# Where five residual loads stand in ScalarE's queue: ahead of the left scan instead of behind its first steps, in layer 1 of a scan-convolution kernel

## The chip, the cores and the metric

One Trainium2 chip, one of its cores. The metric is the device time of one execution in microseconds (us). The kernel before takes 4293.07 us, the median of 3 runs (4291.05 to 4299.52). The core has five engines that run by themselves: TensorE (PE), VectorE (DVE), ScalarE (ACT), GpSimd (POOL) and SyncE (SP). SP and ACT also issue the DMAs here, each in its own order.

## The reference

The input is x, 32 images of 48 channels, 64 rows and 128 columns, float32. Two layers of the same form follow each other; each adds to x a chain of four scans over the group-normalised x.

```python
x = x + conv_ref(_gn(x), down_w, down_b, right_w, right_b, left_w, left_b)

def conv_ref(x, ...):
    # one step of a scan: nxt = inp + conv1d(carry, w, b), 5 taps, 48 -> 48 channels
    D = scan down the rows of x          # 63 steps, conv along the columns
    U = scan up the rows of D            # 63 steps, the same weights
    R = scan right over the columns of U # 127 steps, conv along the rows
    L = scan left over the columns of R  # 127 steps
    return L
```

A step needs the one before it, so the work is a chain of 2 x (2 x 63) steps per image by rows and 2 x 127 by columns and layer.

## The kernel before, in words

The 32 images are four groups of 8. The work is cut into twelve phases (`PHASES`): a phase by rows scans one group down and up (126 steps), a phase by columns scans a pair of groups right and left (254 steps). The order is written out by hand; layer 1 is phases 4 and 7 to 11. Phase 9 is `rows` of layer 1, group 3; phase 10 is `cols` of layer 1, pair 0; phase 11, the last, is `cols` of layer 1, pair 1. Here are 8 x 126 + 4 x 254 = 2024 steps in a row. A step is nine products on PE (`step`, L741) and three additions on DVE, each from PSUM with the bias and the new input, in place into the arena (L750).

The arena in SBUF has three slots and four further tiles (`stage`). A phase by columns works on quarters of 32 columns: a quarter is loaded (`load_unit`, from the DRAM tiles `upa`/`upb`, into which the phase by rows moved its up-going rows with `move_rows`) in six units, 20 DMAs in all. A unit is 128 partitions by 2048 elements, 1 MB, and takes 3 or 4 DMAs, as it is put together from the pieces of several column offsets. Quarters 0, 1 and 2 have a slot each; quarter 0 is spilled to DRAM (`spill_unit`) when it is done, quarter 3 takes its slot, and quarter 0 is brought back in the left scan.

In the left scan a quarter's result is final for this layer when the scan has passed it. Then, unit by unit, POOL adds the residual (`add_residual`, L673), POOL and ACT copy the sum in another order of elements into the tile that held the residual (`permute_unit`, L698), and the tile is stored to the output, or in phase 10 for three quarters to a DRAM tile `held` (`hold_result`, on ACT's queue), from which it goes to the output in phase 11 (`let_result`, on SP's). The residual of a unit is read by `load_residual` from the DRAM tiles `mid`, in layer 1 on ACT's queue, into a ring of tiles: the four stage tiles and one (`spare_tiles[0]`), in the last phase two, that lies in the tile `early`. There it lies on the weights of the phases by rows (`down1`), which are in use up to the end of phase 9; the second lies on the weights of the right scan.

What sets the order. Each piece of work is put on an agenda with a due step (`at(t, fn, ...)`); before each scan step all that is due is issued, in order of due step, by `in_order`, which ties the instructions of each engine into one fixed order. For phase 10 or 11, `t0` is the step at which it begins, `left = t0 + 127` the first step of its left scan. A tie by order is not a time: an instruction runs when its engine has come to it and its waits are over, so ACT, which is not busy in layer 1's right scans, can be far ahead of the steps. In `plan_cols` stands therefore, at `left + 10`, a copy of a single element by ACT (`nc.scalar.copy` to `junk`, shown in the profile under L240) that reads a column which the left scan writes in its seventh step; what is behind it on ACT has to wait for that. The first residual units are put on the agenda at `left + 16`, behind it.

Each DMA of SP and ACT counts up one of eight completion counters, in turn, as the scheduler that builds the program places them. A later DMA on the same counter is issued only when the one before it has landed.

Of the kernel before, what the change touches and what calls it, by code (L numbers as in the profile page):

```python
# [120 lines left out]
def kernel(  # L121
# [508 lines left out]
    def quarter(k, j):  # L630
        return slot[slots(k)[j % 3]].rearrange("p (o s n) -> p s o n", s=2, o=NG)
# [188 lines left out]
    def at(t, fn, *args):  # L820
        agenda.append((t, len(agenda), fn, args))
# [66 lines left out]
    def plan_cols(k, t0, prev):  # L888
        _, layer, pair = PHASES[k]
# [24 lines left out]
        left = t0 + W - 1  # L914
# [20 lines left out]
        for u, (t, j, i) in enumerate(direct):  # L935
            nat = tiles[u % n]
            o, half = UNITS[i]
            if u < n:
                at(left + 16, load_residual, k, j, i, nat)
            if layer == 0:  # L940
                if u >= n:
                    at(direct[u - n][0] + 3, load_residual, k, j, i, nat)
                at(t, add_residual, k, j, i, nat)
                at(t + 4, keep_result, k, j, i)
                unit = quarter(k, j)[:, half, o]
                if half == 0:
                    for b in range(GB):
                        at(t + 5 + b, stats[0].take, j, o, unit, b)
                else:
                    at(t + 1, stats[1].take, j, o, unit)  # L950
            else:

                at(t, add_residual, k, j, i, nat)
                at(t + 2.5, permute_unit, k, j, i, nat, (nc.gpsimd, nc.scalar, nc.scalar))
                if final or j not in HELD:
                    at(t + 4.5, store_result, k, j, i, nat)
                else:
                    at(t + 4.5, hold_result, j, i, nat)
                if final and j == 1:
                    at(t + 4.7, load_residual, k, 0, i, last_tiles(k)[i])  # L960

                if u >= 2 and u - 2 + n < len(direct):
                    at(t + 4.6, load_residual, k, *direct[u - 2 + n][1:], tiles[(u - 2) % n])
# [15 lines left out]
    def last_tiles(k):  # L979

        s = slot[slots(k)[2]].rearrange("p (i n) -> p i n", i=2 * NG)
        return [s[:, i] for i in range(2 * NG)]
# [13 lines left out]
    for k, (kind, layer, _) in enumerate(PHASES):  # L996
        (plan_rows if kind == "rows" else plan_cols)(k, starts[k], PHASES[k - 1][0])
# [211 lines left out]
```

## Time and profile before

| | |
|---|---|
| median of 3 runs | 4293.07 us (4291.05 to 4299.52) |
| the profiled execution, its own time | 4290.3 us |
| its span, first to last instruction | 4288.2 us |
| mean granted clock of PE | 0.981 |
| `arena<-mid` on ACT's queue, 384 KB | 76 DMAs, 9.3 us to landing |
| `early<-mid` on ACT's queue, 384 KB | 20 DMAs, 12.8 us to landing |
| `arena<-upb` on SP's queue, 384 KB | 96 DMAs, 12.3 us to landing |

Times are from the span's start. "Busy" is the time in which an engine has an instruction; a queue (SPq, ACTq) is the issuing side of an engine, and a line of it gives the start, the time up to the last issue, and the number of DMAs. Behind an arrow stands what ended a wait. In a table of stretches the last columns are the granted PE clock, the mean busy share of the 16 DMA engines (a little over 1 is possible) and what they moved in GB/s.

### The profile page before, as it was taken

Reading aid. Unit: us, or ns where it says so; the run is one execution under the profiler, and the core shown is the slowest. Engines: PE = TensorE matmul, PEld = TensorE weight load, DVE = VectorE, ACT = ScalarE, POOL = GpSimd, SP = SyncE. Lnnn points to the kernel's source line nnn. Section 1 sums busy time; section 2 is a strip of 40 time slices with the busy share of each in tenths; the row PEclk is TensorE's granted clock in tenths of the full one; section 3 lists DMA queues with packets and bytes.
Section 4 is the critical chain, followed back from the end, with each engine's and each line's share of the span. In section 5 each row is a group of like instructions: output and inputs, shape, how many; then the busy total and the mean of one; then the engine's idle time right before and its main releaser. Section 6 shows DMA issues by size and latency. Waiting matters only on the chain. (4 is left out here: it accounts for less than half of the span.)

```text
span 4288.2 us, 89979 instructions
## 1 busy us (share of the span) xinstructions
PE 4058.9 (95%) x36648; PEld 4029.3 (94%) x36648; DVE 2164.5 (50%) x6503; ACT 1340.1 (31%) x2662; POOL 886.2 (21%) x906
## 2 busy tenths in 40 slices
PE   3699998999999999998999999999999999999992
PEld 1699998999999999998999999999999999999992
DVE  6345444446664444444446654444444444444443
ACT  1584301435793564100006772613000002210122
POOL 4271001325323020010005310000000024510352
PEclk9899999999999999999999999999999999999996
DMA  9599799857998979679308979939289049999999
GB/s 213 113 216 162 105 167 168 245 127 213 230 198 156 163 140 160 103 127 206 85 1 242 222 154 149 148 50 161 43 140 200 1 78 247 247 243 156 180 202 182
DMA packets 2116733, 680.12 MB, mean 159 GB/s; under 512 B 2005440, under 2 KB 2056160, under 8 KB 2076384
## 3 DMA queue, kind: packets, MB, share of 16 engines
q1 hardware_dynamic: 2015904, 581.64, 70.2%
q10 hardware_dynamic: 97216, 86.44, 9.9%
q0 software_dynamic: 3200, 6.30, 0.5%
q8 instruction: 288, 4.72, 0.5%
q14 instruction: 125, 1.02, 0.1%
HBM read 397.38 MB, written 295.98 MB: 162 GB/s over the span
## 5 line engine op out<-in xcount | busy, mean ns | idle before, releaser
L614 ACT ACTIVATE arena<-arena,offset,scale 128x256 f32<-128x256 f32 (+2 forms) x816 | 575.6, 801 | 432.9 <-DMA arena<-mid 176.1
L673 POOL TENSOR_TENSOR arena<-arena 128x2048 f32<-128x2048 f32 x80 | 363.1, 4553 | 1386.0 <-PE step_10l L741 434.1
L569 POOL COPY arena<-arena 96x256 f32<-96x256 f32 x448 | 265.0, 650 | 553.8 <-DMA arena<-in_x 444.2
L512 ACT ACTIVATE early<-arena 128x256 f32<-128x256 f32 x192 | 129.4, 674 | 477.2 <-POOL arena L673 471.2
L741 PE MATMUL step_00r<-arena,early 128*128 128x128 f32 x2286 | 251.5, 274 | 14.1 <-DMA arena<-upa 14.1
L741 PEld LDWEIGHTS step_00r<-arena,early 128*128 128x128 f32 x2286 | 251.1, 185 | 14.5 <-issue 14.4
L741 PE MATMUL step_01r<-arena,early 128*128 128x128 f32 x2286 | 250.6, 273 | 14.4 <-DMA arena<-upa 14.4
L741 PEld LDWEIGHTS step_01r<-arena,early 128*128 128x128 f32 x2286 | 250.4, 185 | 14.6 <-issue 14.5
L741 PE MATMUL step_11r<-arena,early 128*128 128x128 f32 x2286 | 251.3, 273 | 8.2 <-DVE arena L750 8.2
L741 PEld LDWEIGHTS step_11r<-arena,early 128*128 128x128 f32 x2286 | 250.8, 185 | 8.7 <-DVE arena L750 8.6
L741 PE MATMUL step_00l<-arena,wleft 128*128 128x128 f32 x2286 | 249.1, 272 | 0.0
L741 PEld LDWEIGHTS step_00l<-arena,wleft 128*128 128x128 f32 x2286 | 248.6, 184 | 0.0
L741 PE MATMUL step_10l<-arena,wleft 128*128 128x128 f32 x2286 | 248.5, 272 | 0.0
L741 PE MATMUL step_11l<-arena,wleft 128*128 128x128 f32 x2286 | 248.5, 272 | 0.0
L741 PE MATMUL step_01l<-arena,wleft 128*128 128x128 f32 x2286 | 248.4, 272 | 0.0
L741 PE MATMUL step_10r<-arena,early 128*128 128x128 f32 x2286 | 248.4, 272 | 0.0
L741 PEld LDWEIGHTS step_10l<-arena,wleft 128*128 128x128 f32 x2286 | 248.4, 184 | 0.0
L741 PEld LDWEIGHTS step_11l<-arena,wleft 128*128 128x128 f32 x2286 | 248.4, 184 | 0.0
L741 PEld LDWEIGHTS step_01l<-arena,wleft 128*128 128x128 f32 x2286 | 248.4, 184 | 0.0
L741 PEld LDWEIGHTS step_10r<-arena,early 128*128 128x128 f32 x2286 | 248.4, 184 | 0.0
L698 ACT COPY arena<-arena 128x256 f32<-128x256 f32 x172 | 99.7, 656 | 411.5 <-POOL arena L673 162.2
L240 ACT COPY early<-arena 128x1 f32<-128x1 f32 x2 | 0.4, 191 | 657.9 <-DVE arena L750 657.9
(189 smaller groups left out, 7171.3 us busy)
## 6 DMA issues: line engine op xcount, KB each, us to landing
arena<-in_x SPq DMA_DIRECT2D x24, 1536.0 KB, 11.6
xin<-arena SPq DMA_DIRECT2D x96, 384.0 KB, 4.7
arena<-xin SPq DMA_DIRECT2D x96, 384.0 KB, 8.5
mid<-arena SPq DMA_DIRECT2D x96, 384.0 KB, 7.8
arena<-mid SPq DMA_DIRECT2D x192, 192.0 KB, 4.2
upb<-arena SPq DMA_DIRECT2D x192, 192.0 KB, 3.9
arena<-upb SPq DMA_DIRECT2D x96, 384.0 KB, 12.3
arena<-xin SPq DMA_DIRECT2D x186, 192.0 KB, 4.3
```

The lines of the kernel that those rows point to most:

```text
L240: fn(*args)
L512: nc.scalar.activation(junk[:, 0:n], view[:, b], AF.Identity, accum_out=self.sum[:, i, j : j + 1])
L569: copy(dst[:, r, q], src[:, r0 + r, q])
L614: nc.scalar.activation(args[0], args[0], AF.Identity, bias=args[2], scale=args[1])
L673: eng.tensor_tensor(unit, unit, nat, ALU.add)
L698: copy(by_w(perm)[:, a], src[:, a])
L741: nc.tensor.matmul(part(whole(ps[o])[0:m], -s), weights[:, i, at : at + m], part(src(i), s), start=seen[o] == 1, stop=seen[o] == left[o],)
```

## The change

In layer 1 the first five residual units of each left scan get another due step: unit u of 0 to 4 is due at `left - 44 + 4 * u`, that is at `left - 44`, `- 40`, `- 36`, `- 32` and `- 28`, instead of `left + 16`. This holds for phases 10 and 11. They come thereby ahead of the copy of one element in ACT's order. In phase 10 these are all that fill the ring for the first time; in phase 11, whose ring has six tiles, the sixth stays where it was. Layer 0 stays as it was. Nothing is added or left out.

```diff
             nat = tiles[u % n]
             o, half = UNITS[i]
             if u < n:
-                at(left + 16, load_residual, k, j, i, nat)
+                soon = layer and u < 5
+                at(left - 44 + 4 * u if soon else left + 16, load_residual, k, j, i, nat)
             if layer == 0:
```

The line numbers in the text are those of the kernel before.

## The prediction

> **What bounds the kernel now.** I read the page's busy shares first: TensorE (PE) holds the path. The profiled execution's span is 4288.2 us of its 4290.3, and only about 229 us of it are not PE.
>
> ```profile
> PE 4058.9 (95%) x36648; PEld 4029.3 (94%) x36648; DVE 2164.5 (50%) x6503; ACT 1340.1 (31%) x2662; POOL 886.2 (21%) x906
> ```
>
> The chain that ended last names nothing but the last copy, so I went by stages instead. From VectorE's add that ends each scan step I counted the steps: phase 9 (rows of layer 1, image group 3) ends at 3203.7 us, phase 10 (columns, pair 0) at 3700.3, phase 11 (columns, pair 1) at 4208.1; a column step takes 1.955 us. Then PE's waits: in layer 1's column phases PE waits once.
>
> ```profile
> PE step_11r L741 <- DVE arena L750: 8.2, 1, 8.2
> ```
>
> So a gain can come from that 8.2 us or from the last 80 us alone. What the change touches is the queues, so I read those: what SP's queue waits for, SP's and ACT's DMA issues in order of time, and busy time by stretch (columns: us, then PE, PEld, DVE, ACT and POOL busy, clock, DMA share, GB/s).
>
> ```profile
> SPq L231 <- DMA arena<-mid: 166.9, 1, 166.9
> ```
> ```profile
> 2939.74 41.48 SPq L231 DMA_DIRECT2D upb<-arena  x40
> 2981.32 25.04 SPq L231 DMA_DIRECT2D arena<-upb  x20
> ...
> 3092.24 73.18 SPq L231 DMA_DIRECT2D upb<-arena  x50
> 3165.52 13.77 SPq L231 DMA_DIRECT2D arena<-upb  x14
> 3180.05 19.00 SPq L231 DMA_DIRECT2D upb<-arena  x10
> 3199.16 3.17 SPq L231 DMA_DIRECT2D arena<-upb  x6
> 3202.42 27.71 SPq L231 DMA_DIRECT2D upb<-arena  x20
> 3230.23 23.70 SPq L231 DMA_DIRECT2D arena<-upb  x20
> 3263.44 6.78 SPq L231 DMA_DIRECT2D spill<-arena  x6
> 3270.33 32.39 SPq L231 DMA_DIRECT2D arena<-upb  x20
> ```
> ```profile
> 3464.81 0.19 ACT L240 COPY early<-arena 128x1 f32<-128x1 f32 x1 [505.05 <-DVE arena L750]
> 3464.82 14.41 ACTq L231 DMA_DIRECT2D arena<-mid  x14
> 3479.74 4.66 ACTq L231 DMA_DIRECT2D early<-mid  x3
> ```
> ```profile
> 3018.00:3090.00 72.00, 72.00 (x659) 72.00 (x658) 34.80 (x110) 0.00 (x0) 0.51 (x1) 1.00 0.01 1
> 3165.00:3213.00 48.00, 48.00 (x441) 48.00 (x440) 23.65 (x74) 0.00 (x0) 0.00 (x0) 1.00 1.03 180
> 3213.00:3267.00 54.00, 54.00 (x500) 54.00 (x500) 26.41 (x83) 0.00 (x0) 0.00 (x0) 1.00 0.99 186
> ```
>
> The reader is to see four things. Phase 10's quarter 0 (20 loads `arena<-upb`) is issued by 3006; then SP waits for phase 9's up-going rows and moves them out from 3092 on (80 moves `upb<-arena`), with quarter 1 (14 + 6 loads) between them, in use from step 32. From 3165 to 3267 the DMA engines are full. ACT idles 505 us ahead of the one-element copy of line 971; then its five residual units follow. And the 166.9 us: SP, done at 3302.4, waited until 3469.3, when ACT's first residual load landed (3469.6). Nothing in the data ties an output store to that load: the tie is a completion counter. In the built program all of SP's and ACT's DMAs take turns on eight counters, in the order in which the scheduler placed them, and a queue waits, before it issues, for the previous DMA of that counter, whoever issued it. In before this wait was free, as SP had nothing to do.
>
> **The change part by part.** It moves 17 loads (5 units) in each of phases 10 and 11 from behind the line-971 copy to ahead of it on ACT's queue; none is added. Nothing paces them then but data and counters.
>
> *Phase 10, units 1 to 4 (14 loads).* The built order of after has them right behind ACT's last scaling of phase 9 (2959.8), among the moves of group 2. 5.2 MB, about 28 us (ACT's burst at 3464.8 landed by 3493), push quarter 0 from 3018 to about 3045; it is needed at 3203.7 and the DMA share there is 0.01. Cost 0; without that idle time it would cost up to 28 us.
>
> *Phase 10, unit 5 (3 loads).* Its tile lies on layer 1's down weights, so ACT waits with it for phase 9's last matmul, at about 3203.2. ACT has nothing behind it. But in the built order quarter 0's 20th load, on SP, takes the same counter right after unit 5's first load, and waits for its landing. Behind it on SP stand all 80 moves of group 3 and quarters 1 to 3. So SP, which moved on at 3092, stands until about 3208.
>
> Stall A, at phase 10's first step: unit 5's first load lands 4.8 us after issue (3464.82 to 3469.58, the same size out of an idle queue), then quarter 0's last load 5.2 us after its own (3199.16 to 3204.37): with 0.3 us of issue PE resumes at about 3213.5, a gap of 9.8. To this comes the clock. PE's wait of 8.2 us cost 10.7: that step took 10.24, the next two 3.89 and 2.45 instead of 1.955.
>
> ```profile
> 3833.94 11.23 PE L741 MATMUL step_11r<-arena,early 128*128 128x128 f32 x81 [8.25 <-DVE arena L750]
> ```
> ```profile
> 3834.00:3840.00 6.00, 6.00 (x35) 6.00 (x36) 1.81 (x6) 0.00 (x0) 0.00 (x0) 0.62 0.98 209
> ```
>
> So 2.5 us go on top; PE clock 0.62 in the row after. The Trainium skill (TensorE: Matmul & The Clock Gate, Part 1: The HAM clock gate) has half rate until about 3.4 us of busy time have passed, an estimated 1.7 us per stall; I keep the row's 2.5. A = 9.8 + 2.5 = 12.3 us (9 if loads land faster, 16 if they share the engines).
>
> Stall B, at step 32. SP issues quarter 0's last load at 3208 and then, without its old pacing: 40 moves at the pace of the saturated row, 41.48/40 = 1.04 us each, 41.5 us; 3 us for what is left of unit 5 and quarter 0 (some 0.9 MB at 240 GB/s); then 14 loads, 10 moves and 6 loads as in before under full engines, 3165.5 to the last landing at 3212.7, 47.2 us. Quarter 1 is complete at 3299.7. Step 32 would end at 3203.7 + 12.3 + 32 x 1.955 = 3278.6. PE is freed about 1 us after the landing, and pays the clock again: B = 3300.9 - 3278.6 + 2.5 = 24.8 us (15 with moves at 0.8 us, 32 with moves at the 1.15 us of 3092 to 3103.5).
>
> Quarters 2 and 3 then make it: quarter 2 landed 53.8 us after quarter 1 in before (3266.5), so at 3353.5, while step 64 comes at 3366; quarter 3 another 49 us later, 3402, against 3428. Both margins (12 and 26 us) hide the rest, and are what is late next if B grows less than the moves do.
>
> A rule speaks against this cost. The Trainium skill (DMA: Bandwidth & Descriptors, Issuing engines are not separate DMA queues) says that DMAs of all engines run on the same 16 DMA engines and interleave, and that a second queue saves only issue time. By that alone the moved 5 units are bandwidth in an idle stretch and phase 10 costs 0. The 166.9 us row shows the coupling that it leaves out: one queue standing still on another's DMA. I go by the row.
>
> *Phase 10, left scan.* In before the five units had landed by 3493 and the DMA engines idled from 3500 to 3520, ahead of POOL's first add at 3514. That they are loaded earlier brings nothing: the full stretch from 3520 on begins in the same state. Gain 0; the stalls shift all of it alike.
>
> *Phase 11, units 1 to 5.* ACT reaches them behind its last result store at 3819.8, while quarter 2's last unit is on its way on SP (issued 3819.8 to 3823.5, landed 3833.4; this is the 8.2 us wait). The built order gives them alternate counters with quarter 2's end and quarter 3. They stand behind the 1 MB store on ACT's ring, which landed at 3832.8, so I take 1 us; at full sharing 1 MB at 250 GB/s is 4. Quarter 3 landed at 3868; with 5.2 MB beside it, at 186 GB/s, it lands at about 3896, and step 96 comes at 3899: 0 taken, up to 6 in the range. The copies of held results behind slip by 28 us, from an end at 3998 to one at about 4020, still ahead of the first store at 4029, and the ACT loads that stood there (3976 to 4017) are gone. The last 80 us (DMA share 1.30) move the same bytes: 0.
>
> Sum: 12.3 + 24.8 + 1 = 38 us, on the profiled 4290.3: 4328. The median of the runs is 2.8 above the profiled execution: 4331.
>
> **The rivals.** *No tie (not slower).* The mechanism is SP's wait at quarter 0's 20th load; it decides at 3092, when SP would move on in before. If ACT's unit 5 load is issued or counted so that SP passes by then, A and B vanish, and the five units leave the left scan's queue; at best phase 11's single wait with its clock goes, 10.7 us: 4282 to 4293. For it: the engines are idle where 14 of 17 loads go. Against: the built order has the counter, and before already shows such a wait. 8%.
>
> *Only A.* If moves run much faster than 1.04 us, or quarter 1 lands by 3278, PE waits once: 4293 + 13 = 4306. Against: 3165 to 3267 is full already at 150 to 186 GB/s with half of the moves done. 8%.
>
> *More falls late.* If moves and loads share worse than in sequence, quarter 2 misses step 64 (12 us), and in phase 11 quarter 3 misses step 96 and quarter 2 grows by 4: 38 + 10 to 25, 4341 to 4356, most likely 4348. For it: margins of 12 and 3 us. Against: nothing but bytes is added there. 18%.
>
> **How the numbers follow.** Likeliest (66%): 4331, own range 4318 to 4342 from the ends of A and B, which do not all fall together. For 8 in 10 I take in only A at its upper part and most of the last rival: 4310 to 4351. A change under 0.2% (8.6 us) cannot be told from none by a measurement of this kernel. Faster by more: 4% (the rival without a tie with its whole gain); within: 4%; slower: 92%.
>
> **What would show it.** Right: in the changed kernel's DMA issues SP stands between quarter 0's 19th and 20th load until about 3208, with a wait of about 165 us for a DMA `early<-mid`; the first move of group 3 comes at 3208 instead of 3092; PE has two new waits in phase 10, of about 10 us for `early<-mid` or `arena<-upb` at 3203 and of about 20 us at about 3279, and a clock of 0.5 behind each; phase 10 is 37 us longer, phases 0 to 9 and the last 80 us are unchanged. ACT's first 14 loads are issued from 2960 on. Wrong: moves of group 3 at 3092; a step 32 without a wait; a phase 11 that loses more than 10 us or wins the 8.2.

## The result, and the profile after

The kernel with the change takes 4342.53 us, the median of 4 runs (4333.52 to 4350.06). The kernel before took 4293.75 us beside it (4 runs, 4291.05 to 4299.52). The ratio is 1.011, with a 95% interval from 1.0091 to 1.0129: 48.8 us more, where 38 were forecast. The profiled execution of after took 4343.96 us, with a span of 4342.2. The first view is PE's busy time and its three waits in layer 1's phases by columns (what PE waited for: us in total, times, longest).

```profile
PE 4066.5 (94%) x36648; PEld 4036.5 (93%) x36648; DVE 2165.5 (50%) x6503; ACT 1340.3 (31%) x2662; POOL 885.6 (20%) x906
```
```profile
PE step_10r L741 <- DVE arena L750: 29.0, 1, 29.0
...
PE step_11r L741 <- DVE arena L750: 15.2, 1, 15.2
...
PE step_10r L741 <- DMA upb<-arena: 8.7, 1, 8.7
```

PE's busy time grew by 7.6 us, the span by 54.0: PE mostly stands. Before had one such wait, of 8.2 us in phase 11. Now phase 10 has two and that of phase 11 is nearly twice as long. The names behind the arrows need a second look. The 29.0 us are put down to VectorE's add of step 32, but that add had itself waited 29.3 us, until the last load of quarter 1 landed at 3313.87. The 8.7 us are put down to a move, though PE resumed at 3220.4 us, just after quarter 0's 20th load had landed (3220.2). SP's queue shows both: first what it waited for between 2990 and 3460 us, then its DMAs in order of time (start, us up to the last issue, number).

```profile
SPq L231 <- DMA early<-mid: 182.5, 2, 181.6
```
```profile
3007.02 209.54 SPq L231 DMA_DIRECT2D arena<-upb  x20
3216.67 50.99 SPq L231 DMA_DIRECT2D upb<-arena  x50
3267.76 13.76 SPq L231 DMA_DIRECT2D arena<-upb  x14
3281.98 18.82 SPq L231 DMA_DIRECT2D upb<-arena  x10
3300.90 2.96 SPq L231 DMA_DIRECT2D arena<-upb  x6
3303.96 27.63 SPq L231 DMA_DIRECT2D upb<-arena  x20
```

The 20 loads of quarter 0, 25 us of issue before, now take 209.5, as SP stands for 181.6 us in front of the last one, for a DMA `early<-mid`. The 80 moves of group 3 begin at 3216.67 instead of 3092.24. ACT's queue has the other end of that wait.

```profile
3211.59 1.26 ACTq L231 DMA_DIRECT2D early<-mid  x3
3516.30 0.19 ACT L240 COPY early<-arena 128x1 f32<-128x1 f32 x1 [547.53 <-DVE arena L750]
```

Unit 5's three loads were issued at 3211.59, at the end of phase 9 (3212.0). The first landed at 3216.24 and SP went on at 3216.25. The copy of one element has nothing behind it any more that anyone needs soon. What the two stalls cost is seen in stretches (us, PE, PEld, DVE, ACT and POOL busy, clock, DMA share, GB/s).

```profile
3203.00:3212.00 9.00, 8.78 (x80) 8.59 (x79) 4.61 (x15) 0.00 (x0) 0.00 (x0) 1.00 0.00 0
3212.00:3224.00 12.00, 3.56 (x17) 3.59 (x18) 0.70 (x2) 0.00 (x0) 0.00 (x0) 0.61 0.96 176
...
3285.00:3315.00 30.00, 0.99 (x7) 0.80 (x6) 0.61 (x2) 0.00 (x0) 0.00 (x0) 0.58 1.03 173
3315.00:3325.00 10.00, 10.00 (x69) 10.00 (x69) 3.68 (x11) 0.00 (x0) 0.00 (x0) 0.73 0.95 152
```

The first row is the price of the standing queue: the DMA share is 0.00 just before the data are needed, where before the engines were full from 3165 on. The last shows the clock: PE busy all the time, but 69 products in 10 us, where a full clock makes about 93.

By phases (from the ends of the scan steps, profile of before to profile of after): phases 0 to 9 +8.3 us, phase 10 +43.2, phase 11 +7.1, what follows the last step 80.2 to 75.5. I do not put the first and the last down to the change. Phases 0 to 8 have the same order in both kernels, phase 9 lasts 248.88 us in both, and in the twelve profiles of this study other than that of after the end of phase 9 lies anywhere between 3197.0 and 3209.2 us; the last stretch has between 77.6 and 84.4. The profile of after lies a little outside of both (3212.0 and 75.5), so variation is the likelier reading and not a shown one.

### The profile page after: what moved, and what is told of

Read it like the earlier page. It is cut to its first block, busy times and chain, and to the rows that moved or that the text cites. A ratio compares the mean times of both kernels' runs of the same rounds, so it can differ in the third digit from the quotient of the medians.

```text
span 4342.2 us, 89984 instructions
## 1 busy us (share of the span) xinstructions
PE 4066.5 (94%) x36648; PEld 4036.5 (93%) x36648; DVE 2165.5 (50%) x6503; ACT 1340.3 (31%) x2662; POOL 885.6 (20%) x906
## 3 DMA queue, kind: packets, MB, share of 16 engines
q14 instruction: 125, 1.02, 0.1%
## 5 line engine op out<-in xcount | busy, mean ns | idle before, releaser
L741 PE MATMUL step_01r<-arena,early 128*128 128x128 f32 x2286 | 251.1, 274 | 14.5 <-DMA arena<-upa 14.5
L741 PE MATMUL step_00r<-arena,early 128*128 128x128 f32 x2286 | 250.9, 273 | 14.5 <-DMA arena<-upa 14.5
```

What stands on the lines that cost most here:

```text
L741: nc.tensor.matmul(part(whole(ps[o])[0:m], -s), weights[:, i, at : at + m], part(src(i), s), start=seen[o] == 1, stop=seen[o] == left[o],)
```

## The experiments

Each was timed beside the kernel before, on one chip; the difference given is that of the two medians. The first four take the change apart.

**Phase 10 alone.**

```diff
-                soon = layer and u < 5
+                soon = layer and u < 5 and k == 10
```

> The change made in phase 10 alone; phase 11 as in before. Theory (SP stands at quarter 0's 20th load, which shares a completion counter with unit 5's first load, and unit 5 waits for the last matmul of phase 9): the two stalls at steps 1 and 32 of phase 10, together 43 us in the profile of after, come back whole: 4337 us (4333 to 4341), PE waits of about 9 and 29 us, SP's wait of about 180 us for early<-mid. Rival (the 48.8 us are spread: phases 0 to 9 ended 8.3 us later in the profile of after, and phase 11 lost 7): about 4325.

Measured: 4337.2 us against 4291.82, ratio 1.0106 (1.0091 to 1.0122), +45.4. In its profile phase 10 lasts 541.11 us (496.65 before), phase 11 508.07 (507.72). So nearly all of the loss is phase 10's.

**Phase 11 alone.**

```diff
-                soon = layer and u < 5
+                soon = layer and u < 5 and k == 11
```

> The change made in phase 11 alone; phase 10 as in before. Theory (ACT's five units share the engines with quarter 2's last unit, which is what ends the one wait of phase 11): that wait is 15 instead of 8.2 us, +7; whether the 4.5 us which the last stretch was shorter in the profile of after belong to the change is open: 4296 us if they do, 4301 if they do not. Rival (phase 11's +7 was only that execution's, and the prediction's +1 was right): 4294 to 4295 and a wait of 8 to 9 us.

Measured: 4299.92 us, ratio 1.0022 (1.0013 to 1.003), +8.1. Phase 11 lasts 513.86 us, 6.1 more than before, and the last stretch 79.3, so the 4.7 us by which it was shorter in the profile of after are put down to variation. The one wait has grown, and here the arrow names the load itself, for which VectorE's add had waited too:

```profile
PE step_11r L741 <- DMA arena<-upb: 14.5, 1, 14.5
```

**Units 1 to 4 alone, in phase 10.**

```diff
-                soon = layer and u < 5
+                soon = layer and u < 4 and k == 10
```

> In phase 10 alone units 1 to 4 are moved (14 DMAs, 5.2 MB by the full count of five units less unit 5's share), unit 5 stays at left + 16. Theory (only unit 5's tile waits for phase 9, so only unit 5 can hold SP): no wait of SP beyond that of before, moves of group 3 at about 3092, no wait of PE in phase 10: 4294 us (4290 to 4298). Rival (what costs is the bytes that are put into the queues ahead of quarter 0 and the moves): 14 of 17 loads, so about 36 of the 43 us: 4329.

Measured: 4292.06 us, ratio 0.9997 (0.9986 to 1.0008), +0.2. SP moves on as in before (SP's queue):

```profile
3001.48 24.19 SPq L231 DMA_DIRECT2D arena<-upb  x20
3095.04 72.87 SPq L231 DMA_DIRECT2D upb<-arena  x50
```

14 of phase 10's 17 moved DMAs cost nothing: here their bytes fell into a stretch in which the DMA engines were idle in before (share 0.01). The rival that counts bytes is out.

**Unit 5 alone, in phase 10.**

```diff
-                soon = layer and u < 5
+                soon = layer and u == 4 and k == 10
```

> In phase 10 alone unit 5 is moved (3 DMAs), units 1 to 4 stay at left + 16. Theory: unit 5's first load is again issued only after phase 9's last matmul, and quarter 0's 20th load waits for it on the same counter: all of the 43 us, 4337 us (4333 to 4341), with the same two waits. Rival (bytes): 3 of 17 loads, about 8 us, 4302.

Measured: 4337.85 us, ratio 1.0103 (1.0089 to 1.0117), +46.0. Three DMAs make the whole loss (what SP waited for in this kernel, then PE):

```profile
SPq L231 <- DMA early<-mid: 199.0, 2, 198.6
```
```profile
PE step_10r L741 <- DVE arena L750: 30.1, 1, 30.1
...
PE step_10r L741 <- issue: 8.2, 1, 8.2
```

**Unit 5 on a queue with other counters.** Same bytes, same tile, same wait for phase 9's last product; what differs is the queue (a new last argument of `load_residual`; the lines that pass it on are left out here) and so the completion counter.

```diff
-                soon = layer and u < 5
+                soon = layer and u < 5 and k == 10
-                at(left - 44 + 4 * u if soon else left + 16, load_residual, k, j, i, nat)
+                at(left - 44 + 4 * u if soon else left + 16, load_residual, k, j, i, nat,
+                   nc.gpsimd if soon and u == 4 else None)
```

> In phase 10 alone all five units are moved as in the change, but unit 5's three loads go on POOL's queue, whose DMAs have completion counters of their own. Same bytes, same tile, same wait for phase 9's last matmul. Theory (SP stands only because of the shared counter): SP moves on at about 3092, no wait of PE in phase 10, unit 5 lands at about 3215 beside quarter 1's loads: 4292 us (4288 to 4297). Rival (what costs is unit 5's load itself, at the moment when phase 10 begins and the engines are full): 4337, or at least stall A: 4304.

Measured: 4294.87 us, ratio 1.0004 (0.9995 to 1.0012), +2.4. Phase 10 lasts 496.65 us, to the hundredth what it lasted before. SP's and POOL's queues in it:

```profile
3005.22 23.41 SPq L231 DMA_DIRECT2D arena<-upb  x20
3097.75 72.49 SPq L231 DMA_DIRECT2D upb<-arena  x50
```
```profile
3209.11 1.62 POOL L231 DMA_DIRECT2D early<-mid  x3 [123.64 <-PE step_13u L741]
```

The loads are issued at the same moment as in after, at the end of phase 9, for the same reason, and neither SP nor ACT stands behind them. So it is the shared counter, not the load. It is also the case in which phase 10's five units are early without a cost: no gain.

**Fewer moves ahead of quarter 1.** It asks what sizes stall B; the change is made in phase 10 alone.

```diff
+            if k == 9 and h0 == 24:
+                t += 11
             at(t, move_rows, k, h0, h1, True)
```

> As the change in phase 10 alone, and besides phase 9's moves of rows 24 to 31 (10 moves) are put behind quarter 1's loads on SP: 40 moves instead of 50 stand ahead of quarter 1's first load. Theory (stall B is sized by the number of moves between SP's release and quarter 1, each about 1.02 us): B is 10 us smaller, the wait at step 32 is about 20 us instead of 30.9, stall A as it was: 4327 us (4322 to 4331). Rival (the full engines set when quarter 1 lands, whatever the order on SP): 4337, the wait about 30.

Measured: 4328.79 us, ratio 1.0074 (1.0057 to 1.0092), +36.3, against +45.4 for phase 10 alone. SP's queue and PE's waits:

```profile
3213.80 43.55 SPq L231 DMA_DIRECT2D upb<-arena  x40
3257.45 15.25 SPq L231 DMA_DIRECT2D arena<-upb  x14
```
```profile
PE step_10r L741 <- DVE arena L750: 22.9, 2, 21.7
...
PE step_10r L741 <- DMA upb<-arena: 8.8, 1, 8.8
```

Ten moves less ahead of the loads take the longest wait from the 30.9 us of phase 10 alone to 21.7 and leave stall A about as it was (8.8, against 8.3). The other 1.2 us are at step 64, where quarter 2 is now behind the ten moves. The order in the queue sizes B.

**The loads really 44 steps ahead.** A copy of one element makes ACT wait for the right scan.

```diff
+        if layer:
+            j, v, t = (2, 3 * GB, left - 45) if k == 10 else (2, GB, left - 61)
+            at(t, nc.scalar.copy, junk[:, BN - 1 :], quarter(k, j)[:, 0, 0, v - 1 : v])
         tiles = [stage[:, i] for i in range(4)]
```

> The change in both phases, with a copy of one element ahead of the five units that makes ACT wait: in phase 10 for the right scan's column 80 (so that the units are loaded about 44 steps ahead of the left scan, as the change says), in phase 11 for column 64 (when quarter 2 is in). Theory: unit 5 cannot be ahead of SP's loads any more, and in phase 11 quarter 2 has the engines to itself; both costs go: no wait of PE in phase 10, one of about 8.2 us at step 64 of phase 11, 4292 us (4288 to 4297). Rival (loads ahead of the left scan cost by their bytes, beside quarter 3's loads): a wait at step 96 of phase 10 or 11, 4300 to 4310.

Measured: 4298.68 us, ratio 1.0014 (1.0005 to 1.0023), +6.2. Phase 10 is even (496.68 us). Phase 11 lasts 510.53: the copy came too early, as the first third of column 64 is added before the step needs quarter 2's last unit. So it was made again with the last third.

```diff
+            t, j, o, v = (left - 45, 2, 0, 3 * GB) if k == 10 else (left - 59, 2, 2, GB)
+            at(t, nc.scalar.copy, junk[:, BN - 1 :], quarter(k, j)[:, 1 if o else 0, o, v - 1 : v])
```

> As the paced version, but in phase 11 the copy of one element reads column 64 in the last third of the channels (the add of step 64 that itself needs quarter 2's last unit), as in the earlier paced version ACT's loads were still issued at 3826.9 us, while quarter 2's last unit landed up to 3837. Theory (sharing with quarter 2's last unit is all that the change costs in phase 11): ACT's five units are issued only after step 64, the wait is 7 to 9 us, phase 11 lasts 507 to 508 us: 4292 us (4288 to 4296). Rival (loading ahead costs in phase 11 also by itself, beside quarter 3, or by another pairing of the counters in the left scan of phase 10): wait of 10 us or one at step 96, 4296 to 4300.

Measured: 4296.88 us, ratio 1.001 (0.9999 to 1.0021), +4.4, not told from no change, though 0.9 above the range that was expected. Phases 10 and 11 last 496.68 and 508.27 us, the wait is 9.0. The last stretch of this profile is 84.4 us; there the add that POOL has begun ahead of the last step ends 1.4 us after it, where in before it had ended 1.8 us ahead of it. Whether that comes of the pacing or of that execution is open.

**Phase 11 on other counters.** As phase 11 alone, with the five units on POOL's queue.

```diff
-                soon = layer and u < 5
+                soon = layer and u < 5 and k == 11
-                at(left - 44 + 4 * u if soon else left + 16, load_residual, k, j, i, nat)
+                at(left - 44 + 4 * u if soon else left + 16, load_residual, k, j, i, nat,
+                   nc.gpsimd if soon else None)
```

> The change in phase 11 alone, with the five units on POOL's queue (counters of their own) instead of ACT's. It tells apart the two ways in which phase 11's wait can have grown from 8.2 to 14.5 us. If it is the counters (SP's last loads of quarter 2 wait for ACT's residual loads that took the counters between them): the wait is back at 8 to 9, 4292 us. If it is the sharing of the engines with the residual's bytes: it stays at 12 to 15, 4297 to 4300.

Measured: 4302.64 us, ratio 1.002 (1.0011 to 1.0029), +10.2, and the wait is longer still:

```profile
PE step_11r L741 <- DVE arena L750: 18.5, 1, 18.5
```

So taking the counters apart does not bring the wait back, and sharing alone is enough to make it. POOL issued six of its loads (3814.5 to 3817.1 us) before or among SP's last three (3815.8 to 3820.5), and those landed at 3833.4 to 3839.5, 17 to 19 us after their issue instead of 10 to 11 as in before. Counted from the start of phase 11, the last of the three was issued 1.1 us later than in before and took 9 us longer to land. This run has more loads on their way at once than after has, so it does not say that the counters had no part there. But in after none of SP's last three loads stood for a load of ACT, as the 20th load of phase 10 did: the two phases lose by different mechanisms.

**Another tie, already in before.** Looking for why phase 11 has no margin, I found in the profile of before a stretch in which little is moved, and SP and ACT both standing (stretch; what SP waited for from 3735 to 3770; ACT's queue).

```profile
3740.00:3760.00 20.00, 20.00 (x187) 20.00 (x186) 9.75 (x31) 2.88 (x5) 7.79 (x7) 1.00 0.45 115
```
```profile
SPq L231 <- DVE arena L750: 25.6, 1, 25.6
```
```profile
3746.46 21.78 ACTq L231 DMA_DIRECT2D arena<-mid  x4
3768.28 2.88 ACT L698 COPY early<-arena 128x256 f32<-128x256 f32 x5 [25.15 <-issue]
```

SP waits with the spill of quarter 0 until the right scan has left it. ACT's next residual load has the counter of that spill and waits too, until it lands (3764.17). The 25.15 us ahead of ACT's copy are put down to issue: the load in front of it on ACT. By the order of the program the add, the permute and the tile into which a later unit of quarter 2 goes hang on that load. The edit to the kernel before puts the six spills on POOL's queue:

```diff
         else:
-            dma(there, here)
+            dma(there, here, nc.gpsimd if k == 11 else None)
```

> The kernel before, with one edit: phase 11's six spills of quarter 0 go on POOL's queue instead of SP's. In the trace of before nothing is issued from 3746.5 to 3760.2 us, at a DMA share of 0.45: SP waits for the right scan to leave quarter 0 (step 31, 3761 us), and ACT's residual load behind it takes the counter of SP's spill and waits as well, till 3764. If that tie is what makes quarter 2's last unit late (a tie of the same kind as in phase 10), ACT's load goes 14 us earlier and the wait of 8.2 us at step 64 with its clock (10.7 us) goes: 4282 us (4279 to 4287). Rival (the chain of residual, add, permute and load is bound by bytes or by POOL): 4290 to 4293. On the other side: the spills come later, quarter 3 is late at step 96: 4300 or more.

Measured: 4279.24 us, ratio 0.997 (0.9958 to 0.9982), 13.2 below before and faster than both kernels. First the stretch in which PE stood, in before; then that of 3740 to 3760 us and this one in the new kernel:

```profile
3820.00:3834.00 14.00, 5.75 (x54) 5.56 (x52) 2.74 (x9) 0.00 (x0) 0.00 (x0) 0.80 0.85 232
```
```profile
3740.00:3760.00 20.00, 20.00 (x187) 20.00 (x186) 9.62 (x30) 6.14 (x11) 11.65 (x7) 1.00 1.01 313
...
3820.00:3834.00 14.00, 14.00 (x129) 13.83 (x129) 6.79 (x22) 0.00 (x0) 0.00 (x0) 1.00 1.04 191
```

DMA share 1.01 instead of 0.45; quarter 2 is in at 3797.9 us, 24 before it is needed, and PE waits nowhere in phase 11 (497.24 us instead of 507.72). Of the 13.2 us these are 10.5; it is the wait and its clock, as expected. Which of the two standing queues made that wait is not shown. The edit takes the spills out of SP's own queue as well, and frees what stood behind them there: in before SP's next load of quarter 2 came at 3762.18, 27.9 us after the one ahead of it, and here at 3734.88, 6.5 us after. The trace of before speaks for ACT's side: POOL idled for 27.2 us until one of ACT's loads landed (3781.4), and quarter 2's last loads wait for POOL. A run that frees ACT's load alone is missing.

**The change with both costs covered:** unit 5 of phase 10 on POOL's queue, and the spills of phase 11 too.

> The change whole, in both phases, with its two costs covered: unit 5 of phase 10 on POOL's queue (no tie with SP), and phase 11's six spills on POOL's queue (so that quarter 2 is in some 30 us before step 64 needs it and can share the engines with the five units). Theory (the change costs only through the tie and through phase 11's missing margin, and brings nothing in the left scans): no wait of PE in phases 10 and 11, the time of the kernel that has the spills alone: 4279 us (4275 to 4284). Rival (the early loads are worth something once nothing is in their way): 4270 or less. Other rival (5 MB beside quarter 2 or 3 still cost): 4284 to 4290, a wait at step 64 or 96.

Measured: 4286.15 us, ratio 0.9982 (0.9972 to 0.9991), 7.9 below before. Phases 10 and 11 last 496.65 and 497.12 us, as with the spills alone to within 0.2, and PE waits in neither. So the early units cost nothing once nothing stands behind them and quarter 2 has its margin, and they bring nothing either. The median missed the 4275 to 4284 that was expected, and lies in the range of the rival by which the early loads still cost; but the wait of that rival is not there. In the two profiles 5.4 of the 6.0 us between this kernel and the spills alone lie in phases 0 to 9, where the end of phase 9 varies by more than that, and the intervals of the two ratios overlap. So a small cost is not excluded, and none is shown.

## Why the prediction was right, and where its sizes were off

*The tie* (SP stands at quarter 0's 20th load until unit 5's first load has landed): right, and shown. Unit 5 alone makes it (+46.0), another queue with its own counter takes it away (+2.4). The Trainium skill (DMA: Bandwidth & Descriptors, Issuing engines are not separate DMA queues), by which phase 10 would cost 0, holds for units 1 to 4 (+0.2). For unit 5 the row with the long wait was the better guide, as the rule is about engines and not about what a queue waits for.

*Stall A*, 12.3 forecast: step 1 came out 10.6 us longer and the next 0.45, 11.05. The gap was 8.7 instead of 9.8, as quarter 0's last load landed 3.95 us after its issue instead of 5.2; the clock took 2.4 of the 2.5 assumed.

*Stall B*, 24.8 forecast, is the term that was mis-sized: it measured 32.2 (29.05, 1.93 and 1.21 us over three steps). The prediction put "40 moves at the pace of the saturated row" ahead of quarter 1. The row that it had shown itself reads x50 in front of the x14 loads, and x10 and x20 after them. The pace was right: 50 moves in 50.99 us are 1.02 each. Ten moves are 9.5 us more than the 41.5; the 3 us "for what is left of unit 5 and quarter 0" did not appear, and loads took 46.1 us to the last landing (3267.76 to 3313.87) instead of 47.2. Taking ten moves away took 9.2 us off the wait, which shows the term. The rest of B's difference is stall A, 1.25 us shorter, so that step 32 came earlier, and the clock, 3.1 us instead of 2.5.

*Quarters 2 and 3 in time*: right in phase 10 of after, no wait at steps 64 and 96; with ten moves less ahead of quarter 1 and ten more behind it there was one of 1.2 us at step 64, so the margin was thin, as said. The upper end given for B, 32 us "with moves at the 1.15 us", does not follow from its own sum: 40 moves at 1.15 instead of 1.04 us add 4.4, which makes 29. Nor are 0.9 MB at 240 GB/s 3 us, but 3.75.

*Units 1 to 4 at 0* and *no gain in the left scan*: right (units 1 to 4 alone; unit 5 on the other queue, where phase 10 lasts 496.65 us as before). The 5.2 MB set down for units 1 to 4 are those of all five; four are 4.2 MB. In after they push quarter 0's first 19 loads back by 17 us within phase 9, where 27 were forecast, with room to spare.

*Phase 11*, 1 us forecast, measured 6 to 7 by the profiles and 8.1 by the medians. The step that failed is "They stand behind the 1 MB store on ACT's ring, which landed at 3832.8, so I take 1 us". Being behind that store in the queue kept nothing back. In after, ACT issued the store at 3871.8 us and the first residual loads at 3872.2 to 3875.1, beside it. SP's last three loads of quarter 2, issued at 3875.5 to 3878.2, landed at 3885.2 to 3891.7, up to 13.5 us after issue. Counted from the start of phase 11, the last of them was issued 3.2 us later than in before and took 3.6 us longer to land. The late issue has to do with the counters: ACT's loads took every other one, so SP's last six loads had four counters instead of six, and the last three waited each for an earlier load of SP's own. But the run on POOL's counters lost more, not less, so the sharing of the engines is enough to make a wait of this size; how after's 7 us divide between the two is open. The 4 us which the prediction named for full sharing and did not take were the nearer value. Here the same rule of the Trainium skill spoke for the cost, and was passed over. Quarter 3 stayed in time: it landed at 3946.1, and step 96 began at 3955.8.

*Last 80 us at 0*: right as far as the variation lets it be seen. The four other profiles with the change in phase 11 on ACT's queue have 79.3 to 84.4 us, before has 80.2, and the 75.5 of after lie below all others. In all, phases 10 and 11 cost 50.3 us in the profile of after (43.2 + 7.1), and the medians 48.8, for the 38.1 of the sum: 6.1 more in phase 10, 6.1 more in phase 11. The median, 4342.5, lies at the upper end of the likeliest case (4318 to 4342) and the lower end of the rival "More falls late" (4341 to 4356). One part of that rival came true, quarter 2 of phase 11; the missed steps 64 and 96 did not. So the mechanism forecast for phase 10 held, and the number fell short because two terms were too small.

## What to carry to other kernels

A DMA that is put early in a queue but has to wait, for its data or for its tile, is not early; it is a closed gate, and here what stood behind it was not only its own queue but also the one that shared its completion counter. Before a DMA is moved ahead, find what its tile still holds, and who takes its counter next; here a queue with counters of its own took the gated DMA at no cost that could be told from noise. The same look at a trace (a low DMA share, two queues standing at once, one of them for the other's DMA) found a gain of 13 us that the change was not about, though no run shows which of the two queues it came from.

When a queue is released late, count everything that stands ahead of the first DMA that the scan needs, from the order in the queue, not from what is left of the total.

## What the runs showed of the hardware

In after the granted clock was 0.5 for 10.24, 30.72 and 17.07 us around the three stalls. It was still 0.5 for 4.5, 6.1 and 5.0 us after PE had resumed (3220.4, 3314.4 and 3892.4 us), and the steps that follow lost 2.4, 3.1 and 2.6 us, about half of that time. The 3.4 us that the prediction took from the Trainium skill (TensorE: Matmul & The Clock Gate, Part 1: The HAM clock gate), and its estimate of 1.7 us per stall, were too small each time. The same section says that the window of 3.4 us runs freely, so that the change comes sooner or later by where in a window the work begins; the three stretches are 3, 9 and 5 times 3.41 us, which agrees.

A POOL queue without pacing was no remedy for bandwidth: the same five units on it made phase 11's wait 18.5 us instead of ACT's 14.5. Six of their loads had been issued there when SP issued the last one of quarter 2, on ACT three.
